# Every normalisation of the feed-forward as four ScalarE activations, with the shift made by GpSimd right behind its power

## The chip, the core and the metric

The kernel runs on one NeuronCore of a Trainium2 chip, as one launch. Five engines work from their own instruction streams and meet at semaphores: TensorE (PE in the profile, its weight loads PEld), VectorE (DVE), ScalarE (ACT), GpSimd (POOL) and SyncE (SP), which here only issues transfers. The metric is the device time of the launch in microseconds (us), as the median of the runs shown. Before the change it is 7297.42 us (three runs, 7296.62 to 7308.61).

## What is computed

The input is four images of 128 channels and 64 x 64 points. In layer 0 each image is normalised in 32 groups, goes through three 1x1 convolutions with PReLU, and through an attention of 4096 points to 4096 points; the result is added to the input. Layer 1 sees each image as 4096 tokens of 128 channels: a layer normalisation, an attention of 16 heads of 8 on products of cosines, a feed-forward with two layer normalisations, and last a recurrence over all tokens. Cut to the part that the change touches, in the reference's words:

```python
def _ln(v, g, b):
    mu = jnp.mean(v, axis=-1, keepdims=True)
    var = jnp.mean((v - mu) ** 2, axis=-1, keepdims=True)
    return (v - mu) * jax.lax.rsqrt(var + EPS) * g + b
...
attn_out = ctx @ w_comb.T + b_comb
x1 = _ln(x + attn_out, g1, beta1)                      # "v" in the kernel
zf = jnp.cos(x1[..., :NQ_FFN]) * jnp.cos(ry_theta)
h = jax.nn.relu(zf @ w1.T + b1)
ffn_out = h @ w2.T + b2
return _ln(x1 + ffn_out, g2, beta2)                    # "u" in the kernel
...
t = t + _L1_attn_ref(_ln_t(t), ...)                    # "t2" in the kernel
t = t + _L1_ffn_ref(_ln_t(t), W, V, gamma, beta)       # _ln_t(t): "w" in the kernel
```

So the feed-forward of a group of tokens has three normalisations, called v, u and w after the names of their statistics. `_ln_t` has neither gain nor shift; the other two do.

## The kernel before

**Stages.** The four images (n = 0 to 3) are worked one after another. For each there is a convolution stage (`first_stage`), in which layer 0's attention runs, and then an attention stage (`second_stage`) with layer 1's heads. The feed-forward of image n is not a stage of its own: it runs inside the convolution stage of image n + 1. Only the last image's feed-forward stands alone (`third_stage`), after its attention; then the recurrence follows (the "runs" stage). A branch at the end, with a whole second pass ("r"), is taken only when a check on the numbers asks for it.

**What the convolution stage does.** `layer0` goes over 8 chunks of 512 points (`ic`), and in each over 16 pairs of key tiles (`jp`), two pairs at a time. For two pairs PE computes scores (line 391, four instructions each, into one of two PSUM pairs), ACT takes the exponentials (line 399, 128x1024), DVE adds them to the running totals (lines 404 and 407), and PE multiplies the exponentials of the two pairs before with the values (line 414). One such round with nothing else in it takes PE 5.55 us in the trace. After each `weigh` the kernel calls `meanwhile`, which takes one step of two lists of generators: `tokens` (the start of layer 1 for this image) and `feed_forward` (of the image before).

**What sets the order.** In these stages `tc.manual_schedule` covers TensorE, ScalarE and VectorE: their instructions stand in exactly the order in which the Python code issues them. Each `yield` of `feed_forward` therefore says how many rounds lie between two of its steps. GpSimd is not covered, and its order is made by the scheduler. In the last image's feed-forward (`third_stage`) all engines are ordered by the scheduler, and the eight groups run together.

**The feed-forward of a group.** One call of `feed_forward` works on 512 tokens, as 128 partitions by four blocks of 128 channels (`TG` = 4). There are eight calls an image. The steps that matter here, with their lines:

- x1 is loaded and the bias added by GpSimd (992); the attention's result is transposed (277), copied by ACT (995) and multiplied with the combining weights (1000); DVE adds x1 (1002) and gives v.
- `token_stats` (250 to 255): four times `bn_stats` and `bn_aggr` on DVE (253, 254), then `rsqrt`: epsilon is added on DVE (230), and GpSimd raises 128x4 numbers to the power -0.5 (232).
- Two yields later the normalisation itself. For images 0 to 2 it is `normalise` (line 259): four DVE instructions of 128x128. For the last image it is `normalise_act`: DVE makes `less` = -mean * rstd (line 266), and four ACT activations compute scale * x + bias (line 269).
- v: GpSimd multiplies by g1 (1008) and adds the shift (1009). DVE takes the first eight channels (1017), reduces the argument of the cosine (237 to 244), ACT takes the sine (246), then two small products and a ReLU follow (1043, 1046, 1054).
- u: DVE adds (1064), `token_stats`, normalisation, GpSimd multiplies and adds (1069, 1070).
- t2: DVE adds u and x0 (1075), `token_stats`; PE transposes t2 (the matmuls `pt<-ident,t` of line 277), ACT copies the result (1081) and it is stored. The normalisation w writes u's place in `q`; PE transposes it (`pl`), ACT copies it (1154), and one product (1095) takes the statistics of the last layer.

The pools `stats` (four buffers a tag) hold `st`, `mv`, `var`, `rstd` and `less`.

Of the kernel before, what the change touches and what calls it, by code (L numbers as in the profile page):

```python
# [13 lines left out]
ALU = mybir.AluOpType  # L14
# [12 lines left out]
def kernel(  # L27
# [31 lines left out]
    nc = tc.nc  # L59
# [13 lines left out]
    TG = 4  # L73
# [36 lines left out]
    def get(kind, name):  # L110
        if callable(here[kind]):
            return here[kind](name)
        pool, shape = here[kind]
        return pool.tile(shape, F32, tag=kind, name=name)
# [7 lines left out]
    def half_tile(name):  # L122
        return get("half", name)
# [4 lines left out]
    def one_psum(name):  # L128
        return get("ps_one", name)
# [97 lines left out]
    def rsqrt(var, eps, shape, name, pool=small):  # L227

        v = pool.tile(shape, F32, tag=f"var{shape[-1]}", name=f"v_{name}")
        nc.vector.tensor_scalar(v, var, eps, None, ALU.add)  # L230
        r = pool.tile(shape, F32, tag=f"rstd{shape[-1]}", name=f"r_{name}")
        nc.gpsimd.tensor_tensor(r, v, minus_half[: shape[0], : shape[1]], ALU.pow)
        return r

    def cos_steps(dst, arg, k, r):

        nc.vector.tensor_scalar(k, arg, 1.0 / (2 * math.pi), ROUND, ALU.mult, ALU.add)
        nc.vector.tensor_scalar(k, k, ROUND, None, ALU.subtract)
        nc.vector.scalar_tensor_tensor(r, k, -TWO_PI_1, arg, ALU.mult, ALU.add)
        yield  # L240
        nc.vector.scalar_tensor_tensor(r, k, -TWO_PI_2, r, ALU.mult, ALU.add)
        nc.vector.scalar_tensor_tensor(r, k, -TWO_PI_3, r, ALU.mult, ALU.add)
        yield
        nc.vector.scalar_tensor_tensor(r, r, -1.0, r, ALU.mult, ALU.max)
        yield
        nc.scalar.activation(dst, r, AF.Sin, bias=half_pi[: dst.shape[0]], scale=-1.0)

    def token_stats(src, n_tiles, eps, name):

        st = stats.tile([P, n_tiles, 6], F32, tag=f"st{n_tiles}", name=f"st_{name}")  # L250
        mv = stats.tile([P, n_tiles, 2], F32, tag=f"mv{n_tiles}", name=f"mv_{name}")
        for k in range(n_tiles):
            nc.vector.bn_stats(st[:, k, :], src[:, k, :])
            nc.vector.bn_aggr(mv[:, k, :], st[:, k, :])
        return mv, rsqrt(mv[:, :, 1], eps, [P, n_tiles], name, stats)

    def normalise(dst, src, mv, rstd, n_tiles):
        for k in range(n_tiles):
            nc.vector.tensor_scalar(
                dst[:, k, :], src[:, k, :], mv[:, k, 0:1], rstd[:, k : k + 1], ALU.subtract, ALU.mult  # L260
            )

    def normalise_act(dst, src, mv, rstd, n_tiles, name):

        less = stats.tile([P, n_tiles], F32, tag=f"less{n_tiles}", name=f"less_{name}")
        nc.vector.scalar_tensor_tensor(less, mv[:, :, 0], -1.0, rstd, ALU.mult, ALU.mult)
        for k in range(n_tiles):
            at = slice(k, k + 1)
            nc.scalar.activation(
                dst[:, k, :], src[:, k, :], AF.Identity, bias=less[:, at], scale=rstd[:, at]  # L270
            )

    def transposed(src, name, kind="ps_one"):

        pt = get(kind, name)
        for k in range(TG):
            nc.tensor.transpose(pt[:, ts(k, P)], src[:, k, :], ident)
        return pt

    def blocks(ap):  # L280
        return ap.rearrange("p (k e) -> p k e", e=P)

    def row4(bc):
        return bc.unsqueeze(1).broadcast_to([P, TG, P])
# [694 lines left out]
    def feed_forward(im, i, t2_rows, last, final):  # L979


        n, cols = im["n"], ts(i, IC)

        def norm(dst, src, mv, rstd, name):
            if final:
                normalise_act(blocks(dst), blocks(src), mv, rstd, TG, f"{name}{n}_{i}")
            else:
                normalise(blocks(dst), blocks(src), mv, rstd, TG)

        x1 = get("x1", f"fx1_{n}_{i}")  # L990
        nc.sync.dma_start(out=x1, in_=im["x1"][:, cols])
        nc.gpsimd.tensor_tensor(blocks(x1), blocks(x1), row4(bc_bc), ALU.add)
        pt = transposed(blocks(im["q"][:, cols]), f"pc{n}_{i}")
        cT = get("fhalf", f"cT{n}_{i}")
        nc.scalar.copy(cT, pt)
        yield

        pa = one_psum(f"pw{n}_{i}")
        for k in range(TG):
            nc.tensor.matmul(pa[:, ts(k, P)], cT[:, ts(k, P)], wc_sb, start=True, stop=True)  # L1000
        v = get("fhalf", f"v{n}_{i}")
        nc.vector.tensor_tensor(v, pa, x1, ALU.add)
        yield
        mv, rstd = token_stats(blocks(v), TG, 1e-5, f"v{n}_{i}")
        yield
        yield
        norm(v, v, mv, rstd, "v")
        nc.gpsimd.tensor_tensor(blocks(v), blocks(v), row4(g1_bc), ALU.mult)
        nc.gpsimd.tensor_tensor(blocks(x1), blocks(v), row4(fb2_bc), ALU.add)
        yield  # L1010
        yield

        z, zk, zr = (
            small.tile([P, TG, D], F32, tag=name, name=f"{name}{n}_{i}") for name in ("z", "zk", "zr")
        )
        be1_z = be1_bc[:, 0:D].unsqueeze(1).broadcast_to([P, TG, D])
        nc.vector.tensor_tensor(z, blocks(v)[:, :, 0:D], be1_z, ALU.add)
        steps = cos_steps(zr, z, zk, zr)
        for _ in range(3):
            next(steps)  # L1020
        yield
        yield
        next(steps, None)
        yield
        zs = get("fhalf", f"zs{n}_{i}")
        nc.vector.tensor_copy(
            zs.rearrange("p (k r d) -> p k r d", k=TG, d=D),
            zr.unsqueeze(2).broadcast_to([P, TG, P // D, D]),
        )
        yield  # L1030
        yield
        pz = transposed(blocks(zs), f"pz{n}_{i}")
        zT = get("fhalf", f"zT{n}_{i}")
        nc.scalar.copy(zT, pz)
        yield
        yield
        hs = []
        for f0 in range(0, NF, 2):
            phs = [one_psum(f"ph{n}_{i}_{f}") for f in range(f0, f0 + 2)]
            hs.append(get("hT", f"hT{n}_{i}_{f0}"))  # L1040
            for j in range(2):
                rows = ds(32 * (f0 + j), D)
                nc.tensor.matmul(phs[j], f1_sb[rows, :], zT[rows, :], start=True, stop=True)
            for j in range(2):
                bias = fb1_sb[:, f0 + j : f0 + j + 1]
                nc.scalar.activation(hs[-1][:, j, :], phs[j], AF.Relu, bias=bias)
            yield
        yield
        x0 = get("fhalf", f"fx0_{n}_{i}")
        nc.sync.dma_start(out=x0, in_=im["x0"][:, cols])  # L1050
        po = one_psum(f"pf{n}_{i}")
        for k in range(TG):
            for f in range(NF):
                nc.tensor.matmul(
                    po[:, ts(k, P)],
                    hs[f // 2][:, f % 2, ts(k, P)],
                    f2_sb[:, f, :],
                    start=f == 0,
                    stop=f == NF - 1,
                )  # L1060
        yield

        u = im["q"][:, cols]
        nc.vector.tensor_tensor(u, po, x1, ALU.add)
        mv, rstd = token_stats(blocks(u), TG, 1e-5, f"u{n}_{i}")
        yield
        yield
        norm(u, u, mv, rstd, "u")
        nc.gpsimd.tensor_tensor(blocks(u), blocks(u), row4(g2_bc), ALU.mult)
        nc.gpsimd.tensor_tensor(blocks(u), blocks(u), row4(be2_bc), ALU.add)  # L1070
        yield
        yield

        t2 = get("fhalf", f"t2_{n}_{i}")
        nc.vector.tensor_tensor(t2, u, x0, ALU.add)
        mv, rstd = token_stats(blocks(t2), TG, 1e-5, f"w{n}_{i}")
        yield
        yield
        pt = transposed(blocks(t2), f"pt2_{n}_{i}")
        t2T = get("fhalf", f"t2T{n}_{i}")  # L1080
        nc.scalar.copy(t2T, pt)
        nc.sync.dma_start(out=t2_rows[:, cols], in_=t2T)
        norm(u, t2, mv, rstd, "w")
        yield
        yield
        pt = transposed(blocks(u), f"pl{n}_{i}")
        tokens_i = last(n, i, pt)
        yield
        if n != "r":
            token_products(n, i, tokens_i)  # L1090
# [261 lines left out]
    with stage("runs", t2=((P, 2 * IC), 4 * N), half=(HALF, 2 * NS + 2), ps_one=(ONE, 2 * NS)):  # L1352
# [7 lines left out]
        for k in range(2 * NS):  # L1360
            w = half_tile(f"warm{k}")[:, 0 : NN * (C + 1)].rearrange("p (n c) -> p n c", n=NN)
# [28 lines left out]
        with tc.manual_schedule(engines={nc.tensor.engine, nc.scalar.engine}):  # L1390
# [3 lines left out]
            for t in range(-WARM, L):  # L1394
                for k in range(NS):
# [7 lines left out]
                    w = warm[2 * k + t % 2]  # L1403
# [141 lines left out]
```

## Time and profile before

The profile is of one execution, which took 7301.42 us; its span, from the first to the last instruction, is 7299.6 us.

| what | before |
| --- | --- |
| median of three runs | 7297.42 us |
| profiled execution | 7301.42 us, span 7299.6 us |
| mean granted TensorE clock | 0.981 |
| PE busy | 7004.1 us, 96% of the span |
| DVE busy | 6003.5 us, 82% |
| ACT busy | 5911.8 us, 81% |
| POOL busy | 2794.4 us, 38% |
| convolution stage of image 0 (45 to 440 us) | no feed-forward in it |
| convolution stages of images 1, 2, 3 | around 1700 to 2217, 3490 to 4005, 5280 to 5800 us |
| attention stages | the stretches between them, around 1235 to 1275 us each |
| feed-forward of the last image | around 7040 to 7200 us |

A line of the profile names the engine, the source line, the operation and `out<-in` by the tiles' names. "Busy" counts the time in which an engine has an instruction running; PE's matmuls are pipelined, and a busy PE is not PE at its peak. "PEclk" or "granted clock" is the share of TensorE's clock that was granted. Idle time in front of an instruction is put down to what released it ("<-"). Times of a timeline are counted from the span's start.

### The profile page before, as it was taken

What the parts mean: (1) busy time and instruction counts of PE and PEld (TensorE: products, weight loads), DVE (VectorE), ACT (ScalarE), POOL (GpSimd) and SP (SyncE); (2) the same over time, 40 slices, a digit from 0 to 9 for tenths busy, and PEclk for the clock granted to TensorE, in tenths of its full rate; (3) what the DMA queues carried; (4) which work ended last, traced back from release to release, by engine and by line L of the source; (5) the groups of instructions that cost most, each with busy time, mean ns of one, the idle gap of its engine ahead of it and who ended that gap; (6) DMA issues with size and microseconds to landing.
All of it is one profiled execution on the core that took longest, in us unless ns stands there. A gap on an engine that the chain in (4) does not pass through costs nothing. (4 is left out here: it accounts for less than half of the span.)

```text
span 7299.6 us, 224978 instructions
## 1 busy us (share of the span) xinstructions
PE 7004.1 (96%) x93198; PEld 3502.2 (48%) x93198; DVE 6003.5 (82%) x8097; ACT 5911.8 (81%) x11648; POOL 2794.4 (38%) x9837
## 2 busy tenths in 40 slices
PE   8999999999899999999989999999999899999977
PEld 3445555554444555554444455555444355555546
DVE  5678899887778999889676999889877788888974
ACT  4479999995448999999444999999844599999976
POOL 0034444434223454444422354444522344444542
PEclk9999999999999999999999999999999999999988
DMA  0010000000111000000011100000001110000012
GB/s 28 32 35 24 30 20 21 21 23 13 39 41 37 27 21 20 21 23 20 21 34 45 37 21 20 21 26 19 16 26 37 38 37 21 21 26 27 11 59 105
DMA packets 83101, 212.81 MB, mean 29 GB/s; under 512 B 9120, under 2 KB 10432, under 8 KB 81296
## 3 DMA queue, kind: packets, MB, share of 16 engines
q1 hardware_dynamic: 77312, 186.68, 7.5%
q8 instruction: 733, 12.01, 0.7%
q10 hardware_dynamic: 4304, 11.43, 0.4%
q14 instruction: 304, 2.49, 0.1%
q0 software_dynamic: 448, 0.20, 0.0%
HBM read 141.65 MB, written 56.62 MB: 27 GB/s over the span
## 5 line engine op out<-in xcount | busy, mean ns | idle before, releaser
L886 ACT ACTIVATE e<-s 128x1024 f32<-128x1024 f32 (+1 forms) x3480 | 2949.0, 890 | 61.4 <-PE s L874 38.1
L693 DVE STREAM_TRANSPOSE t<-e 128x1024 f32<-128x1024 f32 x2240 | 2586.9, 1208 | 6.3 <-ACT e L886 3.9
L706 PEld LDWEIGHTS misc<-t,mirror 128*32 128x32 f32 x57344 | 1663.1, 110 | 1410.1 <-issue 1347.8
L706 PE MATMUL misc<-t,mirror 128*32 128x128 f32 x57344 | 1995.2, 273 | 27.6 <-DVE later L720 20.9
L886 ACT ACTIVATE xs<-s 128x1024 f32<-128x1024 f32 (+1 forms) x2152 | 1836.6, 894 | 32.9 <-PE s L874 20.2
L693 DVE STREAM_TRANSPOSE t<-xs 128x1024 f32<-128x1024 f32 x1344 | 1558.4, 1208 | 2.2 <-ACT xs L886 0.7
L727 PE MATMUL acc<-e,q_aug 128*32 128x512 f32 x11360 | 1520.9, 607 | 0.0
L874 PE MATMUL s<-queries,keys 32*128 32x512 f32 x9216 | 1217.2, 495 | 3.9 <-ACT e L886 2.9
L769 POOL COPY own<-o 32x36 f32<-32x36 f32 x2048 | 439.2, 214 | 1708.8 <-DVE o L761 1628.5
L399 ACT ACTIVATE p<-s 128x1024 f32<-128x1024 f32 x512 | 497.7, 1022 | 614.6 <-PE s L391 613.9
L414 PE MATMUL acc<-p,asmT 128*128 128x512 f32 x2048 | 979.4, 611 | 0.0
L727 PE MATMUL acc<-xs,q_aug 128*32 128x512 f32 x7072 | 942.2, 605 | 0.0
L407 DVE TENSOR_TENSOR total<-total,p 128x1024 f32<-128x1024 f32 x448 | 567.9, 1268 | 366.5 <-ACT p L399 343.6
L874 PEld LDWEIGHTS s<-queries,keys 32*128 32x128 f32 x9216 | 480.9, 182 | 491.3 <-issue 373.4
L663 POOL COPY mirror<-q 32x128 f32<-32x128 f32 x2048 | 612.6, 299 | 237.8 <-PE misc L706 150.1
L794 POOL COPY other<-turned 32x64 f32<-32x64 f32 x1904 | 450.9, 237 | 628.0 <-DVE turned L784 549.4
L886 ACT ACTIVATION_READ_ACCUMULATOR e<-s 128x1 f32 x2880 | 651.9, 226 | 0.0
L414 PEld LDWEIGHTS acc<-p,asmT 128*128 128x128 f32 x2048 | 363.0, 192 | 524.2 <-issue 519.7
L391 PE MATMUL s<-e,e 64*128 64x512 f32 x2048 | 533.4, 640 | 7.4 <-DVE asmT L305 7.1
L720 DVE TENSOR_TENSOR later<-later,misc 128x128 f32<-128x128 f32 (+1 forms) x576 | 162.7, 282 | 370.8 <-PE misc L706 366.9
L754 POOL COPY by_token<-by_key 32x4 f32<-32x4 f32 x2016 | 380.8, 189 | 85.2
L727 PEld LDWEIGHTS acc<-e,q_aug 128*32 128x32 f32 x11360 | 225.8, 108 | 348.0 <-issue 330.3
(244 smaller groups left out, 4740.1 us busy)
## 6 DMA issues: line engine op xcount, KB each, us to landing
keys<-parts_dram SPq DMA_DIRECT2D x256, 256.0 KB
queries<-parts_dram SPq DMA_DIRECT2D x1024, 32.0 KB
fx<-x_dram SPq DMA_DIRECT2D x64, 256.0 KB
x_dram<-x SPq DMA_DIRECT2D x56, 256.0 KB
xs<-in_x_dram SPq DMA_DIRECT2D x16, 512.0 KB
t_dram<-t2T SPq DMA_DIRECT2D x32, 256.0 KB
t2s<-t_dram SPq DMA_DIRECT2D x16, 512.0 KB
parts_dram<-high SPq DMA_DIRECT2D x28, 256.0 KB
```

Of the source, the lines that this page charges most:

```text
L391: nc.tensor.matmul(s[:, j, :], e2[rows, ts(2 * jp + j, P)], e1[rows, ts(ic, IC)], start=True, stop=True,)
L399: nc.scalar.activation(p, s, AF.Exp)
L407: nc.vector.tensor_tensor(state[ic], state[ic], p, ALU.add)
L414: nc.tensor.matmul(state["acc", ic], asmT[:, ts(2 * jp + j, P)], p[:, j, :], start=jp == 0 and j == 0, stop=jp == NP - 1 and j == 1,)
L663: nc.gpsimd.tensor_copy(wv[ts(a, 32), s, :, :, ts(a, D)], own[ts(s, 32)])
L693: nc.vector.transpose(group["e"][h][:, k, :], es[h])
L706: nc.tensor.matmul(state["acc"][ts(2 * x + h, 32), :], state["w"][:, QT * (s // 4) + TG * x + s % 4, h, :], state["e"][h][:, :, ds(IC * x ...
L727: nc.tensor.matmul(it["in"]["acc"][ts(2 * h + x, 32), :], it["qa"][:, ds((2 * it["tiles"][x] + h) * V, 32)], it["e"][h][:, ts(x, IC)], sta ...
L769: nc.gpsimd.tensor_copy(own[ts(s, 32), ts(x, 4), h, :], ov[ts(2 * h + x, 32), s, :, 0:V])
L794: copy(to[ts(k, 32), h], tv[ts(2 * x + h, 32), k])
L874: nc.tensor.matmul(ss[h][:, x, :], keys[unit[x] // QT].bitcast(F32R)[r, ts(unit[x] % QT, P)], queries[b].bitcast(F32R)[r, :], start=True, ...
L886: nc.scalar.activation(es[h][:, ts(x, IC)] if split else es[h], ss[h][:, x, :] if split else ss[h].rearrange("p x c -> p (x c)"), AF.Exp, ...
```

## The change

All feed-forwards now use the form that the last image had: the normalisation is four ACT activations with scale `rstd` and bias `less`. `less` itself moves from one DVE instruction to two GpSimd instructions of 128x4 (a product of mean and rstd, then a multiplication by -1). And it is made at once behind the power, in the step of the statistics (`norm_factors`), and no longer two yields later, in the step of the normalisation. The layer normalisation in `tokens`, ahead of the attention, keeps its DVE form.

```diff
-    def normalise_act(dst, src, mv, rstd, n_tiles, name):
+    def minus_mean(mv, rstd, n_tiles, name):
 
         less = stats.tile([P, n_tiles], F32, tag=f"less{n_tiles}", name=f"less_{name}")
-        nc.vector.scalar_tensor_tensor(less, mv[:, :, 0], -1.0, rstd, ALU.mult, ALU.mult)
+        nc.gpsimd.tensor_tensor(less, mv[:, :, 0], rstd, ALU.mult)
+        nc.gpsimd.tensor_scalar(less, less, -1.0, None, ALU.mult)
+        return less
+
+    def normalise_act(dst, src, less, rstd, n_tiles):
+
         for k in range(n_tiles):
             at = slice(k, k + 1)
             nc.scalar.activation(
...
-        def norm(dst, src, mv, rstd, name):
-            if final:
-                normalise_act(blocks(dst), blocks(src), mv, rstd, TG, f"{name}{n}_{i}")
-            else:
-                normalise(blocks(dst), blocks(src), mv, rstd, TG)
+        def norm_factors(src, name):
+            mv, rstd = token_stats(blocks(src), TG, 1e-5, f"{name}{n}_{i}")
+            return minus_mean(mv, rstd, TG, f"{name}{n}_{i}"), rstd
+
+        def norm(dst, src, factors):
+            normalise_act(blocks(dst), blocks(src), *factors, TG)
...
-        mv, rstd = token_stats(blocks(v), TG, 1e-5, f"v{n}_{i}")
-        yield
-        yield
-        norm(v, v, mv, rstd, "v")
+        factors = norm_factors(v, "v")
+        yield
+        yield
+        norm(v, v, factors)
...
-        mv, rstd = token_stats(blocks(u), TG, 1e-5, f"u{n}_{i}")
-        yield
-        yield
-        norm(u, u, mv, rstd, "u")
+        factors = norm_factors(u, "u")
+        yield
+        yield
+        norm(u, u, factors)
...
-        mv, rstd = token_stats(blocks(t2), TG, 1e-5, f"w{n}_{i}")
+        factors = norm_factors(t2, "w")
         yield
         yield
         pt = transposed(blocks(t2), f"pt2_{n}_{i}")
         t2T = get("fhalf", f"t2T{n}_{i}")
         nc.scalar.copy(t2T, pt)
         nc.sync.dma_start(out=t2_rows[:, cols], in_=t2T)
-        norm(u, t2, mv, rstd, "w")
+        norm(u, t2, factors)
```

In the built program the order of PE, DVE and SP in the convolution stages is what it was, less the 96 DVE normalisations of each; ACT gets 96 activations a stage at the places where the DVE ones stood, and no table load more. On GpSimd the two new instructions stand behind each power, and the scheduler moves a few of its neighbours: the power of u of some groups now stands behind the two GpSimd passes over v of the next group. In the last feed-forward the order of a few instructions near its end shifts.

## The prediction

> **What bounds the kernel now.** I read the page first (PE 96% busy, DVE 82%, ACT 81%), then busy time by stage, because the change touches only the three convolution stages with a feed-forward in them, and the last feed-forward. Columns: stretch, its length, then busy us (instructions) of PE, PEld, DVE, ACT, POOL, the granted clock, DMA share, GB/s.
>
> ```profile
> 45.00:440.00 395.00, 387.24 (x1344) 156.50 (x1344) 244.08 (x386) 173.79 (x193) 37.34 (x85) 0.99 0.08 26
> 1700.00:2217.00 517.00, 472.72 (x1798) 216.25 (x1797) 367.20 (x778) 224.18 (x259) 151.39 (x197) 0.96 0.11 35
> ```
>
> The stage without a feed-forward leaves PE idle for 7.8 us, the one with it for 44.3 us, at a clock of 0.96. The other two are like it (43.4 and 45.2). ACT is busy 43% of the stage, DVE 71%, so no engine but PE is near its limit over the stage; what costs time is DVE being late for single PE steps. PE's own waits in 1700 to 2220 us (us in total, times, longest):
>
> ```profile
> PE pt L277 <- DVE t L1075: 22.7, 5, 7.8
> PE pl L277 <- DVE q L259: 4.7, 2, 3.4
> PE pq L277 <- DVE z L1017: 2.8, 1, 2.8
> ```
>
> The timeline around the longest shows what stands before t2 in DVE's queue.
>
> ```profile
> 1864.94 1.94 ACT L399 ACTIVATE p<-s 128x1024 f32<-128x1024 f32 x2 [3.61 <-PE s L391]
> 1867.36 1.11 POOL L232 TENSOR_TENSOR r_u<-v_u,minus_half 128x4 f32<-128x4 f32 x1 [8.89 <-DVE v_u L230]
> 1868.72 2.06 DVE L259 TENSOR_SCALAR v<-v,mv_v,r_v 128x128 f32<-128x128 f32 x4
> 1869.31 1.99 PE L391 MATMUL s<-e,e 64*128 64x512 f32 x8
> 1870.48 1.94 ACT L399 ACTIVATE p<-s 128x1024 f32<-128x1024 f32 x2 [3.61 <-PE s L391]
> ...
> 1876.43 1.11 DVE L259 TENSOR_SCALAR q<-q,mv_u,r_u 128x128 f32<-128x128 f32 x4
> ...
> 1881.72 0.94 DVE L1075 TENSOR_TENSOR t<-q,fx 128x512 f32<-128x512 f32 x1
> 1882.72 1.11 PE L277 MATMUL pt<-ident,t 128*128 128x128 f32 x4 [7.79 <-DVE t L1075]
> ```
>
> DVE works without a gap from 1860.44 to 1882.66, and two normalisations lie in that run. The power of u is ready at 1868.47, but DVE reaches u only at 1876.43. ACT stands idle for 3.61 us between pairs of exponentials. Costs of single instructions, from the groups by form (busy, mean ns | idle before):
>
> ```profile
> L259 DVE TENSOR_SCALAR q<-q,mv_u,r_u 128x128 f32<-128x128 f32 x96 | 52.8, 611 | 0.0
> L259 DVE TENSOR_SCALAR v<-v,mv_v,r_v 128x128 f32<-128x128 f32 x96 | 36.0, 438 | 2.0 <-POOL r_v L232 2.0
> L259 DVE TENSOR_SCALAR q<-t,mv_w,r_w 128x128 f32<-128x128 f32 x96 | 26.6, 340 | 3.7 <-POOL r_w L232 3.7
> L269 ACT ACTIVATE v<-v,less_v,r_v 128x128 f32<-128x128 f32 x32 | 13.2, 483 | 16.0 <-DVE less_v L266 11.8 <-DVE st_v L253 4.2
> L748 POOL TENSOR_TENSOR by_key<-by_key,denom 128x8 f32<-128x8 f32 x63 | 12.9, 206 | 4.9
> L232 POOL TENSOR_TENSOR r_v<-v_v,minus_half 128x4 f32<-128x4 f32 x32 | 33.1, 1033 | 326.6 <-DVE v_v L230 324.0 <-DVE zk L237 2.6
> ```
>
> **What the Trainium skill says.** "SBUF — State Buffer", section "Who interferes with whom": VectorE and GpSimd share one port pair; an instruction of VectorE in a two-port mode or with two SBUF inputs and one of GpSimd hold each other up, while ScalarE never waits for a port. The trace agrees: the same four DVE normalisations take 1.11 us, or 3.18 us in front of and beside GpSimd's pass (at 2082.13). "ScalarE: Activation LUTs", section "What ACT_TABLE_LOAD costs": 280 ns + 0.833 ns an element with a pointer bias, 93 ns for a second pointer, an estimate of 480 ns for 128 elements; the trace has 483, which I use. The same page, "Table sets: the hidden batching unit": cheap functions such as identity are in every set; no table load stands at line 269 in the trace, and the built program has as many loads as before. "TensorE: Matmul & The Clock Gate", section "Part 1: The HAM clock gate": after about 3.4 us without work the clock halves until it is busy again. The trace agrees: the four transposes after the 7.79 us wait take 1.11 us, against 0.60 elsewhere.
>
> **Removed from DVE.** 288 normalisations, 52.8 + 36.0 + 26.6 = 115.4 us, 38.5 a stage; and 24 `less` in the last feed-forward. Only what stands before a late PE step counts. The steps of one stage:
>
> - t2 at 1882.72, late by 7.79: v 2.06 + u 1.11 = 3.17 saved.
> - t2 at 1938.27, late by 3.85: v 2.06 (at 1921.72) + u 1.11 (at 1928.84) = 3.17 saved.
> - t2 at 2093.93, late by 5.27: v 1.11 + u 3.18 = 4.29 saved.
> - t2 at 2148.09, late by 5.57: u 1.11 saved; the rest is exponentials that came late, and stays.
> - `pl` at 1945.78, late by 3.45: the power of w is ready at 1941.35, DVE begins at 1945.38. ACT can begin at about 1941.8; its first block is done 0.48 later, about when PE gets there. 3.4 saved. A shorter one (1.29) goes too: its power was ready 4.1 us before DVE began.
> - `pq` at 1824.69, late by 2.8: DVE's products for q stand behind v (2.34) and u (1.80). 2.8 saved, of which I count 2.3.
>
> Sum: 3.17 + 3.17 + 4.29 + 1.11 + 3.4 + 1.29 + 2.3 = 18.7 us a stage. Three of these waits fall below the length that cools the clock; with 1.11 against 0.60 for transposes and 3.6 against 1.99 for the scores behind them, one cold start costs about 2 us. I count one, 2 us, since the others may be cold for another reason.
>
> **Added on ACT.** 96 activations a stage, 4 x 0.483 = 1.93 us a normalisation, 46 us in all, into a stage with 293 us of idle ACT. What decides is whether the exponentials behind them come too late. A round without other work is 5.55 us (scores start at 1863.76 and 1869.31). The first exponential of a pair ends 1.02 us after 1864.94, and PE wants its PSUM again at 1869.31: spare 3.35 us (2 us where a table load of 1.28 us stands before it). For all 24 normalisations I took from the timeline when ACT is free, when the power ends, and when the next exponentials or their load begin; the normalisation ends 1.93 us after the later of ACT free and power + 0.4. Five cause no delay, thirteen (pairs as one) delay the next ACT work by 0.3 to 3.0 us, and two by more. Group 4's v: ACT is free at 1717.60, the power ends at 1722.36, so it ends at 1724.7 instead of exponentials at 1721.21, 3.5 late. Groups 3's v and 2's u together: u's power ends at 2082.06, ACT is done at 2084.4 instead of 2078.68, 5.7 late. The delays sum to 34 us a stage; beyond the spare are 0.1 + 2.4, and about 1 at table loads: 3.5 us.
>
> **Added on GpSimd.** 48 instructions of 128x4 a stage, two for each of 24 powers. By the nearest rows (128x8 product 0.206, 32x4 copy 0.189) the two take 0.4 us. No row has a GpSimd multiplication by a constant; the upper bound is that it takes as long as the power, about 1.0 each, and the powers beside DVE's totals take 1.92. With 2.0 us for both, the delays sum to 52 us and about 13 go beyond the spare. Below 0.4 there is nothing to win: the late starts are the powers' own. I take 0.4 to 1.0, and a loss of 4.5 us. GpSimd's own time (151 of 517 us busy) covers them; queued behind are its passes over v and u, for which DVE's t2 waits, and these start up to 8 us earlier than now because ACT doesn't wait in DVE's queue. Where the scheduler puts u's power behind the passes over the next v (groups 6, 7, 2), v is normalised by 1863.2 in group 7, its passes end by 1866.5 to 1867.5, and u's power starts at 1867.36 anyway. No transfer moves past another: SP's order is the same.
>
> **Last feed-forward.** DVE waits 16.6 + 7.2 + 6.6 us in front of `less` and ACT 26.3 us for it; these hops become one. Against it GpSimd, 14 of 20 us busy from 7040 to 7100, gets 48 instructions, 10 us at 0.2 each, 48 at 1.0. I take a gain of 2; the ends are 10 gained and 15 lost.
>
> **Sum.** Each stage 18.7 + 2 - 4.5 = 16.2, three of them 48.6, with the last about 50 us. Against the profiled execution (7301.42, span 7299.6) that gives 7251; the median shown lies 4 lower, so I predict 7248 us.
>
> **Rivals.**
>
> - *ACT's delays reach PE* (slower). The mechanism is the in-order ACT queue: exponentials wait behind a normalisation that waits for statistics, power and `less`, above all at w, right behind PE's transposes of t2. If none of the spare is there, 34 us a stage are lost against 20.7 won: 3 x 13 = 40 us slower, 7337; with GpSimd's upper bound more. It decides above 21 of the 34 us. For it: two delays do exceed the spare, and DVE's totals, which follow the exponentials, start later, so the lateness of t2 can come back. Against it: 3.61 us of idle ACT and 3.35 us of spare in most rounds. 18%.
> - *The lateness only moves* (no change). DVE's saving is eaten because its idle time is in waiting for exponentials (DVE totals wait 83.2 us for them in this stage), which now come later; 16 us shrink to under 5 a stage: 7283 to 7312. 14%.
> - *More is won.* With DVE never behind, the 33 us that PE waits for t2, `pl`, `pq` and the like vanish, and five cold starts of 2 us with them, less the 3.5 us that ACT costs: 3 x (33 + 10 - 3.5) = about 119 us, 7178. Against it: t2 at 2148 and half of that at 1882 have other causes. 8%.
> - My forecast: 60%.
>
> **Chances and range.** 0.2% is 14.6 us, about what a measurement of this kernel can tell from no change. Faster 0.68, same 0.14, slower 0.18. The likeliest case alone spans 7225 to 7283. For eight in ten I leave out the best of the third rival and most of the first beyond GpSimd's lower price: 7205 to 7315.
>
> **What would show it.** In the stage at 1700 us: PE's wait for t2 from 22.7 us to about 11, for `pl` to about 0, no line 259 for v, q; ACT busy 270 us, DVE 329; the stage some 16 us shorter. Wrong it would be if ACT shows waits for `less` with PE waiting for exponentials at the scores, if the two GpSimd instructions take over 1 us each, or if t2 is as late as now.

## The result, and the profile after

The changed kernel takes 7284.55 us (median of ten runs, 7277.62 to 7291.59). The kernel before took 7301.95 us beside it on the same chip (ten runs, 7291.36 to 7308.61). The ratio is 0.9978, with a 95% interval of 0.997 to 0.9985: faster by 0.22%, 17 us where 50 were forecast. The profiled execution took 7289.74 us, its span is 7288.0 us, 11.6 us shorter than that of before.

The busy time by stage, with the columns of the prediction's first view:

```profile
45.00:440.00 395.00, 387.25 (x1344) 156.43 (x1342) 243.24 (x383) 173.87 (x193) 37.15 (x84) 0.99 0.08 26
1700.00:2217.00 517.00, 476.66 (x1852) 218.34 (x1854) 338.74 (x691) 266.72 (x369) 166.34 (x247) 0.97 0.11 35
```

DVE has 28 us less in this window, ACT 43 us more, GpSimd 15 us more. (After the change the stage ends some 6 us earlier, so the window holds more of the next one. Over the stage itself, 1707.6 to 2220.5 us before and 1708.6 to 2214 after, DVE goes from 362.9 to 329.7 us: 33 less where normalisations of 38.5 left, because some other DVE instructions got longer.) PE's idle time in the window fell only from 44.3 to 40.3 us. PE's own waits in 1690 to 2220 us (us in total, times, longest):

```profile
PE pt L282 <- DVE t L1081: 12.5, 3, 5.7
PE pc L282 <- ACT hT L1052: 5.4, 7, 0.8
PE s L396 <- ACT p L404: 4.3, 2, 3.2
PE pq L282 <- DVE q L551: 3.6, 2, 1.9
PE pl L282 <- ACT q L274: 2.8, 1, 2.8
PE pq L282 <- DVE z L1023: 2.4, 1, 2.4
...
PE sum L496 <- ACT x L487: 1.6, 1, 1.6
PE pz L282 <- DVE zs L1032: 1.0, 1, 1.0
```

(`pt`, `pq`, `px`, `pz` and `pl` are PE's transposes, `pl` that of the normalised w; `sum` is the product that adds up DVE's totals.) The wait for t2 fell from 22.7 to 12.5 us. New are waits of PE that lead to ACT: the scores `s` for exponentials (4.3), and `sum` for a copy of ACT's (1.6). `pl` now waits for ACT where it waited for DVE. ACT's largest waits in the same stretch say why:

```profile
ACT p L404 <- PE s L396: 111.2, 37, 8.5
...
ACT q L274 <- POOL less_w L267: 18.9, 7, 3.5
ACT q L274 <- POOL less_u L267: 17.5, 4, 7.1
```

With 6.6 us for `less_v` ACT stands 43 us in front of normalisations, and its order is fixed. The groups by form, over the whole execution (busy, mean ns | idle before, what ended it):

```profile
L274 ACT ACTIVATE q<-q,less_u,r_u 128x128 f32<-128x128 f32 x128 | 53.4, 483 | 67.0 <-POOL less_u L267 67.0
L274 ACT ACTIVATE q<-t,less_w,r_w 128x128 f32<-128x128 f32 x128 | 52.7, 483 | 63.3 <-POOL less_w L267 63.3
L267 POOL TENSOR_SCALAR less_u<-less_u 128x4 f32<-128x4 f32 x32 | 15.5, 485 | 2.8
...
L266 POOL TENSOR_TENSOR less_u<-mv_u,r_u 128x4 f32<-128x4 f32 x32 | 10.5, 329 | 2.5
```

An activation costs the 483 ns that was taken. The two GpSimd instructions take 0.8 us together for u and w (0.44 for v), inside the 0.4 to 1.0 taken.

### The account

The waits of PE, summed over the three convolution stages from answers like the one above, with the prediction's terms times three (us):

| term | forecast | before to after | measured |
| --- | --- | --- | --- |
| t2 | 35.2 saved | 68.0 to 36.1 | 31.9 saved |
| `pl` | 14.1 saved | 14.1 to 8.4 | 5.7 saved |
| `pq`, for `z` | 6.9 saved | 8.2 to 7.2 | 1.0 saved |
| `px` | none | 3.7 to 0 | 3.7 saved |
| scores, for exponentials | 13.5 lost | 0 to 12.3 | 12.3 lost |
| `sum`, for ACT's copy of x | none | 0 to 8.0 | 8.0 lost |
| `pq`, for DVE's q | none | 5.5 to 11.3 | 5.8 lost |
| `pz` | none | 0 to 2.8 | 2.8 lost |
| PE busy at half the granted clock, half of it | 6 saved | 93.4 to 96.8 | 1.7 lost |
| last feed-forward | 2 saved | | none (below) |
| sum | 50.7 | | 11.7 |

At half the granted clock the same four transposes take 1.11 us that take 0.60 to 0.66 at the full one; so half of PE's busy time at half clock is counted as lost, as an estimate. The measured terms make up the 11.6 us between the two profiled spans. (Between the medians it is 17; single executions of the changed kernel lie up to 14 us apart.) PE's idle time in the three stages, added up as gaps between matmuls, fell by 13.5 us (132.0 to 118.5); the eight terms of waiting make 13.4. Of the 39 us that are missing from the forecast, 15.4 are losses that weren't counted, 13.9 are savings of waiting that didn't come, 7.7 the clock and 2 the last feed-forward.

Three windows of the timeline show the losses. First, the x copy at 1830 us; start, duration, engine, line, operation, and in brackets the idle time before it and what ended it. Before:

```profile
1830.26 1.28 ACT L399 ACT_TABLE_LOAD   x1 [0.54 <-PE s L391]
1830.55 1.11 DVE L259 TENSOR_SCALAR q<-t,mv_w,r_w 128x128 f32<-128x128 f32 x4 [0.31 <-POOL r_w L232]
1831.56 1.94 ACT L399 ACTIVATE p<-s 128x1024 f32<-128x1024 f32 x2
...
1833.41 0.59 ACT L482 COPY x<-px 128x512 f32<-128x512 f32 x1
1835.03 0.64 PE L491 MATMUL sum<-total,ones 128*32 128x128 f32 x16
```

And after:

```profile
1831.45 0.23 POOL L267 TENSOR_SCALAR less_w<-less_w 128x4 f32<-128x4 f32 x1
1831.71 1.65 ACT L274 ACTIVATE q<-t,less_w,r_w 128x128 f32<-128x128 f32 x4 [1.53 <-POOL less_w L267]
...
1833.38 1.28 ACT L404 ACT_TABLE_LOAD   x1
...
1834.67 1.94 ACT L404 ACTIVATE p<-s 128x1024 f32<-128x1024 f32 x2
...
1836.50 0.59 ACT L487 COPY x<-px 128x512 f32<-128x512 f32 x1
1837.14 0.64 PE L496 MATMUL sum<-total,ones 128*32 128x128 f32 x16 [1.57 <-ACT x L487]
```

The exponentials come 3.1 us later, and the copy behind them too. The scores bear that: PE's next ones start at 1840.59 and wait for nothing. For the copy it is too much. Before, it ended at 1834.00 and PE came to `sum`, which waits for it, at 1835.03: a spare of 1.0 us. After, `sum` waits 1.57. In the other two stages the same wait is 3.2 us each.

Second, u at 2078 us. Before:

```profile
2077.50 1.99 PE L391 MATMUL s<-e,e 64*128 64x512 f32 x8
...
2078.68 1.94 ACT L399 ACTIVATE p<-s 128x1024 f32<-128x1024 f32 x2 [3.61 <-PE s L391]
```

And after:

```profile
2071.89 1.99 PE L396 MATMUL s<-e,e 64*128 64x512 f32 x8
...
2078.06 1.65 ACT L274 ACTIVATE q<-q,less_u,r_u 128x128 f32<-128x128 f32 x4 [7.08 <-POOL less_u L267]
2079.61 1.91 ACT L404 ACTIVATE p<-s 128x1024 f32<-128x1024 f32 x2
...
2080.66 2.04 PE L396 MATMUL s<-e,e 64*128 64x512 f32 x8 [3.16 <-ACT p L404]
```

ACT waits 7.08 us for u's factor and the scores then 3.16 us for the exponentials behind it. This is the delay that the prediction took as 5.7 us, 2.4 beyond the spare. Counted from the start of their scores, the exponentials begin 7.72 us later, before 1.18: a delay of 6.5 us. Less the spare of 3.35 this gives 3.2, what PE waits. So for the scores the spare was right.

Third, DVE's products for q at 2026 us, which PE's `pq` waits for. Before:

```profile
2031.02 0.90 DVE L546 TENSOR_TENSOR q<-q,r 128x64 f32<-128x64 f32 x3
...
2033.08 1.27 POOL L1008 TENSOR_TENSOR v<-v,g_bc 128x512 f32<-128x512 f32 x1 [4.38 <-PE s L391]
```

And after:

```profile
2024.83 2.18 POOL L1014 TENSOR_TENSOR v<-v,g_bc 128x512 f32<-128x512 f32 x1 [1.36 <-ACT v L274]
...
2025.79 3.95 DVE L551 TENSOR_TENSOR q<-q,r 128x64 f32<-128x64 f32 x3
...
2029.89 0.63 PE L282 MATMUL pq<-ident,q 128*128 128x128 f32 x4 [1.67 <-DVE q L551]
```

Before, GpSimd's passes over v and u began behind these products; now v is normalised earlier, the passes lie beside the products, and the products take 3.95 us instead of 0.90.

### The profile page after: what moved, and what is told of

Same layout as the page of the kernel before. It is cut to its first block, busy times and chain, and to the rows that moved or that the text cites. A ratio compares the mean times of both kernels' runs of the same rounds, so it can differ in the third digit from the quotient of the medians.

```text
span 7288.0 us, 225126 instructions
## 1 busy us (share of the span) xinstructions
PE 7006.0 (96%) x93198; PEld 3501.8 (48%) x93198; DVE 5902.5 (81%) x7785; ACT 6018.3 (83%) x11936; POOL 2838.9 (39%) x10029
## 5 line engine op out<-in xcount | busy, mean ns | idle before, releaser
L396 PE MATMUL s<-e,e 64*128 64x512 f32 x2048 | 538.2, 645 | 19.7 <-ACT p L404 12.5
L732 PEld LDWEIGHTS acc<-e,q_aug 128*32 128x32 f32 x11360 | 225.7, 108 | 347.4 <-issue 329.7
```

The source lines that it names most:

```text
L396: nc.tensor.matmul(s[:, j, :], e2[rows, ts(2 * jp + j, P)], e1[rows, ts(ic, IC)], start=True, stop=True,)
L732: nc.tensor.matmul(it["in"]["acc"][ts(2 * h + x, 32), :], it["qa"][:, ds((2 * it["tiles"][x] + h) * V, 32)], it["e"][h][:, ts(x, IC)], sta ...
```

## Experiments

Each ratio is to the kernel before on the same chip. PE idle and half clock are from the profile, summed over the three convolution stages, as in the account.

| kernel | median us | ratio, 95% interval | PE idle | PE busy at half clock |
| --- | --- | --- | --- | --- |
| the change | 7284.55 | 0.9978 (0.997 to 0.9985) | 118.5 | 96.8 |
| no normalisation | 7237.6 | 0.9918 (0.9904 to 0.9931) | 85.9 | 68.6 |
| ready factors | 7262.92 | 0.9947 (0.9934 to 0.9961) | 102.6 | 81.8 |
| more ACT work, before | 7306.56 | 1.0007 (0.9999 to 1.0016) | 133.5 | 111.4 |
| v and u on ACT | 7279.36 | 0.997 (0.9961 to 0.998) | 114.7 | 75.6 |
| w on ACT | 7307.27 | 1.0007 (1.0 to 1.0013) | 135.4 | 96.0 |
| last feed-forward only | 7301.41 | 1.0002 (0.9994 to 1.0011) | | |
| before, no totals | 7157.6 | 0.9805 (0.9792 to 0.9819) | 31.9 | 26.6 |
| the change, no totals | 7163.68 | 0.9813 (0.98 to 0.9826) | 36.7 | 27.3 |
| ready factors, no totals | 7164.78 | 0.981 (0.9797 to 0.9824) | 33.0 | 33.1 |
| v, u, w one step later | 7273.45 | 0.9959 (0.9945 to 0.9972) | 102.9 | 88.6 |
| v, u later, w on DVE | 7278.79 | 0.9968 (0.9956 to 0.998) | 106.0 | 84.7 |
| ready factors, one step later | 7276.49 | 0.9965 (0.9952 to 0.9979) | 101.4 | 97.4 |

### What DVE's relief is worth, and what ACT's waiting and working cost

No normalisation: v, u and w of images 0 to 2 are not normalised at all.

```diff
         def norm(dst, src, factors):
-            normalise_act(blocks(dst), blocks(src), *factors, TG)
+            if final:
+                normalise_act(blocks(dst), blocks(src), *factors, TG)
```

> In the three convolution stages the normalisations of v, u and w are left out (their results are not computed; what follows reads the unnormalised v, u and q); statistics, power and the two GpSimd instructions stay, and the last feed-forward is that of the change. Theory A (the lateness of DVE's steps was worth what was forecast, and ScalarE's queue gives it back): about 18 us a stage or more under the kernel before, so 45 to 70 us faster than it, a ratio of 0.990 to 0.994. Theory B (taking the normalisations off DVE was never worth much to PE, since DVE then only waits for exponentials): not faster than the change itself, so a ratio of 0.997 to 0.999 to the kernel before.

65 us faster by the medians, 60 by the ratio: 20 to 22 a stage. The forecast's 18.7 + 2 a stage for DVE's relief alone is about that; this kernel also drops the normalisations from the chain of each group, so the value is an upper one. And that the totals agree is in part luck: over three stages PE's idle time fell by 46.1 us where 56.1 were counted, and the time at half clock by 24.8, worth some 12.4 where 6 were counted. `pl` doesn't wait any more, but `pz` right behind it now waits 14.6 us where it waited for nothing: as much as `pl` was to save.

Ready factors: the same activations at the same places, with constants for scale and shift. ACT then never waits for GpSimd there, and DVE and GpSimd do what they do in the change. (It still waits 23 us over the three stages for DVE's statistics, which read the tile that it writes.)

```diff
         def norm(dst, src, factors):
+            if not final:
+                factors = (zeros4, ones[:, 0:TG])
             normalise_act(blocks(dst), blocks(src), *factors, TG)
```

> In the three convolution stages the activations take scale and bias from constants (one and zero) that are ready from the start, so they normalise nothing; everything else, with the statistics, the powers and the products on GpSimd, stays as in the change. ScalarE has the same work and no wait for GpSimd. Theory A (what was lost is ScalarE's waiting, 43 us in the first of these stages, with the exponentials queued behind it): 10 us a stage faster than the change, 45 us under the kernel before, ratio about 0.994. Theory C (the 46 us of work on ScalarE itself make the exponentials late): as the change, ratio 0.997 to 0.998. Theory B: the same as the change.

22 us faster than the change: so much does waiting for factors cost beyond that. By PE's idle time it is 16 us (118.5 to 102.6), by the half clock 7.5. The waits name the place: the scores' 12.3 us vanish, `sum` falls from 8.0 to 1.2, `pl` from 8.4 to 0. But t2 doesn't move (36.1 and 38.4), and where `pl` is gone, PE meets the next late step at once (ready factors, the same place as the change's `pl`):

```profile
1938.59 1.08 PE L284 MATMUL pz<-ident,zs 128*128 128x128 f32 x4 [4.46 <-DVE zs L1036]
```

In the change PE waits 2.8 us for `pl` and 1.0 for `pz` there. Over three stages `pz` waits 14.1 us here, 2.8 in the change. So w's wait had been covering DVE's lateness with `zs`, and the 3.4 us forecast for this `pl` were not to be had from w alone.

More ACT work: the kernel before, with four activations more behind each DVE normalisation; they multiply a tensor of weights by one and add `b1`, which is zero in these inputs, so nothing changes, and they wait for nothing.

```diff
             else:
                 normalise(blocks(dst), blocks(src), mv, rstd, TG)
+                if n != "r":
+                    for _ in range(TG):
+                        nc.scalar.activation(
+                            W_sb, W_sb, AF.Identity, bias=b1_sb, scale=ones[:, 0:1]
+                        )
```

> The kernel before, whose DVE normalisations stay; where the change puts its normalisations in the three convolution stages ScalarE gets four activations of 128x128 more that wait for nothing (they copy a weight onto itself). This is the added ScalarE work by itself. If the spare of 3.35 us a round is real in the sense of the forecast (later exponentials inside it are free), the time is that of before, at most 2 us a stage more: ratio 1.000 to 1.001. Theory A2, formed after the runs that left out the normalisations or their waits (the exponentials' lateness comes back through DVE's running totals, so ScalarE's work costs about 8 us a stage even without a wait): 20 to 27 us slower, ratio 1.003 to 1.004.

5 to 6 us slower, with an interval that begins at no change and ends at 12 us. So 46 us of ACT work a stage cost about 2 us a stage, and not the 20 to 27 us in all of theory A2: that ACT's work itself eats the gain is out. PE's waits grow by little (the scores' to 1.3 us, `sum`'s to 1.9), so the rule of the spare holds for work that doesn't wait. The added work stands in blocks of 2.1 us, in four places of the first stage of 4.2; longer delays weren't tried in this way. In its profiled execution, the slowest of its runs, PE is at half clock 18 us longer than before.

### Which of the normalisations

v and u on ACT, w as before on DVE; and the other way round. (The two differ in the letters.)

```diff
+            if not final and name not in "vu":
+                return None, mv, rstd
...
+            if factors[0] is None:
+                normalise(blocks(dst), blocks(src), *factors[1:], TG)
```

> In the three convolution stages v and u are normalised by ScalarE as in the change, w by DVE as before; the last feed-forward is that of the change. Theory A: ScalarE's waits for the factors of w (18.9 us in the first stage, right in front of exponentials) go, while the savings ahead of t2 stay: 3 to 6 us a stage faster than the change, ratio about 0.996. Theory B: between before and the change, 0.998 to 0.999.

> In the three convolution stages only w is normalised by ScalarE, v and u by DVE as before; the last feed-forward is that of the change. Theory A: t2 stays as late as before (22 us a stage), and the waits for the factors of w come on top: no faster than before, ratio 0.999 to 1.002. Theory B: also about 1.000. If w was what won the time (transposes of w that waited 4.7 us for DVE), the ratio is 0.998.

v and u alone give as much as the whole change or a little more, less than the 3 to 6 us a stage over it that theory A expected: the waits for w's factors are gone, but `pl` is back (16.9 us), and the scores still wait 10.6. w alone gives nothing, perhaps a small loss. In w's kernel the wait `pl` falls from 14.1 to 4.5 us over three stages, and `sum` (6.3) and `pz` (2.8) come up in its place, with 2.5 more at `pwx`, which reads ACT's next copy: 9.6 won, 11.6 lost.

The last feed-forward alone, with the three stages as before:

> The change in the last feed-forward alone: there GpSimd makes the shift behind its power; in the three convolution stages DVE normalises as before. Forecast: 2 us faster than before (10 faster to 15 slower). From the traces of before and after (160.4 and 161.0 us from the last exponential to the recurrence): no difference, ratio 0.9995 to 1.0005.

No difference (1.0002, 0.9994 to 1.0011). Neither end of the forecast's range, 10 gained or 15 lost, is within the interval. Its gain of 2 us isn't seen, but so small a gain can't be told from none by these runs.

### Is it DVE's totals that make everything late?

The running totals (DVE's line 407, 412 after) are left out but for the first addition of each chunk, so most exponentials are missing from the sums:

```diff
-            else:
-                nc.vector.tensor_tensor(state[ic], state[ic], p, ALU.add)
```

> The kernel before with DVE's running totals of layer 0's exponentials left out but for the first addition of each chunk (line 407; the softmax sums are then wrong). It is the reference of the next run. DVE gets some 142 us of work less a stage, so t2 is hardly late: the three stages with a feed-forward shrink by 15 to 35 us each, the first one by little; 50 to 100 us under the kernel before, ratio 0.987 to 0.993.

> The change with the same running totals left out. Without them late exponentials reach PE only by PSUM and by the products that read them. If that alone were the loss (the forecast's rule, 2.5 to 4.5 us a stage, or more if the spare is smaller), this run is slower than the one before it by 8 us or more. If the loss goes through the totals in front of t2's steps (theory A2), it is within 5 us of it, or faster by what is left of DVE's saving.

Without totals the kernel before takes 143 us less, more than the 50 to 100 that were expected. No t2, `pl` or `pq` is late in it (PE idle 31.9 us in three stages), and there the change wins nothing; it is 6 us behind, between the two theories' marks of 5 and 8, with intervals that overlap. In its trace `sum` waits 4.4 us for ACT's copy; in the kernel before without totals it doesn't. So all that the change wins is the lateness of a DVE full of totals.

> Left out: the running totals of DVE in all stages, so the sums of exponentials are wrong, and the factors of the normalisations of v, u and w, so these are copies; everything else is as in the change. Two theories on the 22 us by which the change is behind the kernel with ready factors. Through the totals: ACT waits for GpSimd's factors, exponentials and then DVE's totals come later, and t2 behind them on DVE; without totals nothing is left to be late, so this run is within 6 us of the change without totals (7163.7), that is 7158 to 7166. Directly: the late exponentials keep PE from its scores, whatever DVE does; then about 20 us stay to be won without totals too, and the time is 7140 to 7150.

The number is the one of the first theory: without totals, ready factors are worth nothing (7164.78 against 7163.68). The trace makes that theory narrower. Without totals, the change's ACT has hardly a factor to wait for, in 1690 to 2220 us:

```profile
ACT v L274 <- POOL less_v L267: 4.3, 1, 4.3
ACT q L274 <- POOL less_w L267: 1.0, 1, 1.0
ACT q L274 <- POOL less_u L267: 0.2, 1, 0.2
```

That is 5.5 us against 43.0 with totals. The totals stand before the statistics in DVE's queue, late statistics make late powers, and ACT waits for these. What ACT's waiting then costs goes straight to PE, by scores, copies and `pl`, since ready factors leave t2 as late as in the change. "Exponentials late, so totals late, so t2 late" does happen (DVE's totals wait 378 us for exponentials in the three stages, 284 before, 337 with ready factors), but no gain in t2 comes of taking it away.

### One step later

If ACT stands in front of a normalisation because the factor isn't there, the normalisation can be issued a step later, behind that step's exponentials. For v and u one more yield before it (and before GpSimd's passes), one fewer behind; for w one of the two yields behind it is put ahead.

```diff
         factors = norm_factors(u, "u")
         yield
         yield
+        yield
         norm(u, u, factors)
...
         yield
-        yield
...
-        norm(u, t2, factors)
         yield
+        norm(u, t2, factors)
         yield
```

> The change with v, u and w normalised one step (half a round, some 2.8 us) later, at the cost of one of the two steps that follow each of them; the whole feed-forward is as long as before in steps. ScalarE then meets factors that are ready more often. If ScalarE's waits for the factors are most of what was lost (the run with ready factors was 22 us faster than the change), this wins a good part of it: 7266 to 7278 beside 7303 for the kernel before, ratio 0.995 to 0.997. If the later products on GpSimd make t2 late instead, it is as the change or slower: 0.998 to 1.000.

> v and u on ScalarE one step later as in the other run, w on DVE at its old place. Ratio 0.995 to 0.996 if both gains add (w on DVE gave 0.997 to 0.9978 of the change); about 0.997 if the later step only trades one wait for another.

With all three a step later the time is 7273.45 us, 11 us under the change and 27 under the kernel before: the best complete version here. Its interval and the change's touch at 0.997, so the gain over the change is likely rather than certain by these runs. PE's idle time is 102.9 us, that of ready factors; the waits of the scores (12.3) and of `sum` (8.0) are gone. ACT still waits 55 us for factors in the three stages (130 in the change), and `pl` still waits 8.5. The wait for DVE's q falls too, from 11.3 to 7.3, where GpSimd's passes now meet DVE's products later (these take 3.00 us in the first stage instead of 3.95). So the gain isn't ACT's waiting alone. The timeline at the place of the first window, in this kernel:

```profile
1831.29 1.28 ACT L404 ACT_TABLE_LOAD   x1 [0.53 <-PE s L396]
1832.59 1.94 ACT L404 ACTIVATE p<-s 128x1024 f32<-128x1024 f32 x2
...
1834.45 0.59 ACT L487 COPY x<-px 128x512 f32<-128x512 f32 x1
1834.99 1.65 ACT L274 ACTIVATE q<-t,less_w,r_w 128x128 f32<-128x128 f32 x4
```

The copy now stands ahead of w, and here w waits for nothing. The price is at t2, which GpSimd's passes reach later: 45.8 us of waiting against 36.1. With v and u alone a step later the time is 7278.79 us, no different from v and u unmoved (7279.36).

> Left out: the factors of the normalisations of v, u and w of images 0 to 2, which here are copies; all else as in the version with v, u and w one step later (7273.5). If that version is good because ACT no longer waits for factors, nothing is left to gain and the time is within 5 us of it, 7268 to 7276. If it is good because GpSimd's passes over v and u lie beside other instructions of DVE, and waits remain, both gains add: 7250 to 7258. If one step later is only a part of the waits, the time is that of ready factors without the step, about 7263.

7276.49 us, within 3 us of the late version with true factors and with the same idle time (101.4 against 102.9). Once the normalisations stand a step later, the waiting for factors that is left costs nothing that these runs can show. Against ready factors without the step it is 14 us slower at the same PE idle time (102.6). Half of its extra time at half clock, 97.4 against 81.8 us, is 8 us of that; why PE is at half clock longer, and the other 6 us, stay open.

## Why the prediction was wrong

**What held.** That it gets faster, by relief of DVE in front of late PE steps, with ACT's waiting as the counter-weight. t2: 31.9 us saved of 35.2 (in the first stage 2.1, 3.9, 3.2 and 0.8 at the four places, where 3.2, 3.2, 4.3 and 1.1 were counted). Scores: 12.3 us lost of 13.5, in the first stage at the two delays that were named in advance, 1.15 and 3.16 us; that the sum agrees is in part luck, since 0.1 and 2.4 were counted there, and the rest for table loads and GpSimd's price, which cost the scores nothing. The prices of the activations and of GpSimd's pair. ACT busy 267 us for 270; DVE 339 for 329, half of the ten because the window holds more of the next stage.

**The step that failed: "The delays sum to 34 us a stage; beyond the spare are ..., 3.5 us".** The losses are 28.9 us over the three stages, not 13.5. The spare was worked out for one consumer, PE's scores, which have two PSUM pairs. Everything behind a normalisation in ACT's queue is delayed, and the copies of PE's transposes, which have less spare, were put at nothing. In the first window the copy came 3.1 us later and had 1.0. (By the prediction's rule the scores' spare is 2 us there, because of the table load, so its "about 1 at table loads" may stand for this place; but the scores lost nothing, and the copy did.) Over the three stages `sum` lost 8.0 us. With ready factors it waits 1.2, in the version with all three a step later not at all: so ACT's waiting is the cause for `sum` and the scores.

The 5.8 us at `pq`, for DVE's q, have another cause, which the prediction didn't count either: GpSimd's passes over v, which follow v to its earlier place (third window). This wait, 1.4 to 1.7 us a stage, is there in the three kernels with totals whose passes lie beside the whole of these products (the change, v and u on ACT, ready factors). At this place it is absent where v stays on DVE or isn't normalised, and with v a step later, where the products take 3.0 us in the first stage, it is 0.7 us or less. It makes 4.9 of the 5.8 us. The 2.8 us at `pz` are the next point.

**Savings counted at places with a second late step.** `pl` was to save 14.1 us and saved 5.7. The wait at 1945.78 was 3.45 us and is 2.82 after. For one part the factor came later than the 0.4 us behind the power (the timeline of after):

```profile
1936.58 1.11 POOL L232 TENSOR_TENSOR r_w<-v_w,minus_half 128x4 f32<-128x4 f32 x1 [6.57 <-DVE v_w L230]
1937.77 0.30 POOL L266 TENSOR_TENSOR less_w<-mv_w,r_w 128x4 f32<-128x4 f32 x1
1937.93 2.55 DVE L412 TENSOR_TENSOR total<-total,p 128x1024 f32<-128x1024 f32 x2
1938.16 1.08 POOL L267 TENSOR_SCALAR less_w<-less_w 128x4 f32<-128x4 f32 x1
1939.27 1.65 ACT L274 ACTIVATE q<-t,less_w,r_w 128x128 f32<-128x128 f32 x4 [3.37 <-POOL less_w L267]
```

The power ends at 1937.69 and ACT starts at 1939.27, 1.6 us later, because the second small instruction takes 1.08 beside DVE's totals (0.23 elsewhere). For another, PE comes to `pl` earlier. The wait for t2 just before, 3.85 us, is gone, and the transposes and products between run at the full clock, in 0.66 and 1.88 us instead of 1.11 and 3.15. So PE stands at `pl` 0.7 us before w's power is ready, where before it came 1.0 us after it: the cold start that was saved went into the next wait. And `pz` was late right behind. `pq` for `z` was to save 6.9 and saved 1.0; the normalisations are gone from DVE before it, but at 1818.32 DVE waits 3.25 us for exponentials that ACT gives 2.3 us later than before.

**t2 at 1882 saved 2.1 of 3.17.** v is now normalised early, so GpSimd's passes over it start at 1865.05, where before v was only normalised by 1870.78, and they run beside other DVE work. Before and after:

```profile
1862.91 1.11 DVE L259 TENSOR_SCALAR x<-x,mv_t,r_t 128x128 f32<-128x128 f32 x4
...
1865.03 3.23 DVE L259 TENSOR_SCALAR x<-x,mv_t,r_t 128x128 f32<-128x128 f32 x4
1865.05 1.27 POOL L1014 TENSOR_TENSOR v<-v,g_bc 128x512 f32<-128x512 f32 x1 [3.86 <-ACT v L274]
```

The four instructions take 2.1 us more. The Trainium skill, "SBUF — State Buffer", section "Who interferes with whom", has the shared port pair as an exclusive lock, held for a whole instruction; the trace agrees, in that the first two of the four end within 0.1 us of the end of a GpSimd pass (1866.40 and 1867.75 behind 1866.32 and 1867.67), but no run took this collision away by itself. In the same run of DVE work one step of r also got longer (0.69 to 1.63), while z and `zk`, which collided before, got shorter (1.29 to 0.18 and 1.12 to 0.18). So collisions moved, and their net cost here is 1.1 us. The prediction used that rule to price a normalisation leaving DVE, and not for the pass that follows it to its new place. Its sentence "u's power starts at 1867.36 anyway" fell with it: it starts at 1871.60, of which 2.1 us are this collision and 2.1 the shift of everything there against before.

**The clock.** One cold start less a stage, 2 us, was counted, from waits that fall below the length that by the prediction halves the clock. PE's waits over that length did get fewer, from 15 to 6 in the three stages, but its busy time at half clock went from 93.4 to 96.8 us. The length of single waits doesn't decide it: without totals the kernel before has no PE wait over 1.8 us in these stages and is still at half clock for 26.6 us of work. At 1840.76 in that run the clock is halved for 3.4 us, with no wait over 0.77 us in the 8 us before, and the scores take 3.59 us instead of 1.99. What does decide stays open. The time at half clock moves by several us between kernels with the same idle time, as the last experiment shows, and should have been left at nothing with a wider range.

**The rivals.** "ACT's delays reach PE" has the mechanism right and decides where more is lost than won; lost are 9.6 us a stage, won 14.1. "The lateness only moves" gave 7283 to 7312 for what was measured, 7284.55, but by an account that is right in part only: at `pl` and `pz`, and at DVE's q, lateness did move, but t2's went, and most of the gain was given back at ACT's copies and the scores. "More is won", 119 us, is more than the 65 that leaving the normalisations out altogether gives.

## What to carry to other kernels

When work is put into an in-order queue, list every instruction behind it up to the next idle time, with the consumer of each: the spare of the double-buffered one is not the spare of a copy that PE's very next step needs. Free capacity is cheap to use (46 us of extra ACT work a stage cost about 2), but an instruction that waits for an operand costs the waiting too; put it behind the work that is ready, as the version with one step later does. A late step behind another late step is not saved by mending the first. And work that follows a step to its new place, as GpSimd's passes follow v, meets other work there: look at what it will lie beside.

## What the runs showed of the hardware that was not expected

A GpSimd instruction on 128x4 numbers, 0.20 to 0.23 us alone, took up to 1.27 us beside DVE's totals. Four DVE normalisations of x took 3.23 us beside GpSimd's passes, 1.11 without them, and three DVE products of 128x64 took 3.95 beside them, 0.90 without. TensorE's clock was halved after waits no longer than 0.77 us. And three kernels with PE idle times of 101.4 to 102.9 us in these stages differ by up to 13.6 us in their medians, some of which is time at half the granted clock (81.8 to 97.4 us).
